# A float32 attention kernel: the transfers of each row maximum are issued by GpSimd instead of SyncE

## The chip, the cores and the metric

The kernel runs on one core of one Trainium2 chip. The metric is the device time of one execution in microseconds (us). Of the kernel before, three timed runs are shown: 7329.24, 7341.15 and 7340.35 us, median 7340.35 us. One more execution was recorded by the hardware profiler. All durations in this document come from that profile unless something else is said.

The engines have short names in the profile: PE is TensorE's matmul, PEld its weight load, DVE is VectorE, ACT is ScalarE, POOL is GpSimd and SP is SyncE. A name with a q behind it (SPq, POOLq) is the engine's queue: issues of transfers and waits for semaphores.

## The reference

The input is x, 4096 rows of 256 numbers, normalised to xn. Two blocks read xn, and the result is x plus both.

The first block is an attention with 16 heads of 16 numbers. It takes most of the time, and the change is in it:

```python
attn = einsum('bqhd,bkhd->bhqk', q, k)
sq = attn * attn
nsum = (qn + kn).transpose(0, 2, 1)[..., None]   # squared lengths of q and k
w = softmax(sq / (nsum - 2.0 * sq + EPS))        # over all 4096 keys
out = einsum('bhqk,bkhd->bqhd', w, v).reshape(B, S, D)
return out @ wo + bo
```

Each of 16 heads has 4096 x 4096 scores, and each score goes through a square, a quotient, an exponential and a matmul with v. The softmax needs the maximum of every row of 4096 scores before its exponential.

The second block has two layers of local attention (8 heads, windows of 128) and a gated feed-forward network. It is called the chain here, since each of its steps follows the one before.

## The kernel before, in words

**Tiles.** The attention is worked in 512 tiles (16 heads x 32 blocks of 128 queries). A tile `i` has 128 queries on the partitions and 4096 keys, in two halves `n = 2i` and `2i + 1` of 2048. A half goes through these methods of the class `Acts`:

- `scores` (L951, PE) and `square` (L955, ACT): products in PSUM, squared into the tile `r`.
- `less` (L959, DVE): subtracts a constant from `r`.
- then the reciprocal of `r` by way of logarithm and exponential: `positive` (L972, DVE), `log` and `power` (L978 and L981, ACT); in some tiles the two halves share one reciprocal, with `product` (L963) and `signed` (L985) on DVE.
- `weights` (L993, DVE): the quotient, and its maximum along the row. After the second half, the maximum over all 4096 keys of each query stands in one column of the small tile `mm` (128 partitions x 1 number).
- `maximum` (L997 to L1007): prepares that maximum for PE. It is the function that is changed.
- `turn` (L1014 and L1017, PE): for each stretch of 512 keys, first a matmul (L1014) that writes minus the row's maximum into PSUM, from the row tile `mrow`; then four transposes (L1017) that add the quotients to it.
- `exp` (L1025, ACT) and `values` (L1036, PE): the exponential of that, and its matmul with v.

**What `maximum` does.** For the matmul L1014, the maxima of 128 queries must lie as a row, along one partition, and in bf16 without loss. So each is split into three bf16 parts. A part is the upper half of the 32-bit number, which `head` shows as bf16; GpSimd subtracts the part from the number (L1007), and the upper half of the rest is the next part. Two subtractions make three parts. Each part, a column of 128 partitions with 2 bytes each, is moved by a transfer (L1004) into one row of `mrow`: row 0, 1 and 2. There are four such tiles (`M_ROWS = 4`), used in turn. Before the change, the transfers are issued by SyncE, in this order for each tile: transfer of part 1, subtraction, transfer of part 2, subtraction, transfer of part 3.

**The order of the work.** PE, ACT and DVE follow an order that a planner (`Plan`, `plan_all`) writes out before the program runs, with a cost in ns for every step; an engine works through its list in order and waits where something isn't there yet. The planner takes `maximum` as 6 us that lie on no engine (`MAX_NS = 6000.0`, "X"): it places a tile's `turn` no earlier than 6 us after the end of its `weights`. The steps of the chain fill the gaps. GpSimd and SyncE have no planned list: they take what the program gives them, in the order of the program, each in its own queue.

**What else lies in these two queues.** SyncE issues nearly all transfers: loads of queries, keys and values of a head (L338, L328, L332), the stores of results (L1045), and the loads and stores of the chain. GpSimd works, besides L1007, for the chain's local attention: in `looked`, four instructions (L745 to L748) split the maxima of a window into bf16 parts in the same manner, 128 times; SyncE moves those (L751) to the row tile `frow`, which PE reads at L760. There are a few fills with constants (L605, L625 to L627, L636) too.

The changed function, as the profile's line numbers have it:

Of the kernel before, what the change touches and what calls it, by code (L numbers as in the profile page):

```python
# [272 lines left out]
def tile_yat_attention_and_local_ffn(ctx: ExitStack, tc: tile.TileContext, io, out):  # L273
    nc = tc.nc
# [648 lines left out]
    class Acts:  # L923
# [74 lines left out]
        def maximum(self, i):  # L998

            mm = self.mm.pop(i)  # L1000
            head = mm.bitcast(BF)
            self.mT[i] = mT = mrow[i % M_ROWS]
            for c_ in range(1, 4):
                nc.sync.dma_start(mT[c_ - 1:c_, :], head[:, 2 * c_ + 1:2 * c_ + 2])  # L1004
                if c_ == 3:
                    break
                G.tensor_tensor(mm[:, c_ + 1:c_ + 2], mm[:, c_:c_ + 1], head[:, 2 * c_ + 1:2 * c_ + 2], ALU.subtract)  # L1007
# [217 lines left out]
```

## Time and profile before

| | |
|---|---|
| timed runs, median of 3 | 7340.35 us (7329.24 to 7341.15) |
| the profiled execution, its own time | 7328.83 us |
| the profiled execution, its span from first to last instruction | 7327.0 us |
| busy: PE, DVE, ACT, POOL | 6747.6, 6907.5, 6972.8, 1806.4 us |
| granted TensorE clock, mean | 0.981 |
| attention tiles from the first L1004 (262.8 us) to the last (7298.7 us) | 512, one in 13.7 us |
| transfers `mrow<-mm` | 1536, of 0.2 KB each |
| instructions L1007 | 1024, 1010 ns in the mean |

How to read it: the first 260 us are a prologue that makes q, k and v. From there on, three engines are busy over 90% of the time, and the chain's work is spread over nearly the whole span. So no single engine's sum is the time; each us in which one of the three waits can show in the end. A mean duration on POOL holds the time in which an instruction had begun and was held up, as the shortest (189 ns) and the longest (11197 ns) of L1007 tell.

### The profile page before, as it was taken

The numbers are of one execution on the slowest core, as the hardware profiler recorded it, in microseconds if no ns is written. First come the engines' busy times: TensorE is split into PE (matmuls) and PEld (weight loads), VectorE is DVE, ScalarE is ACT, GpSimd is POOL, SyncE is SP. The second block draws the span as 40 slices with busy tenths as digits, with TensorE's granted clock in tenths as the row PEclk, the third lists the DMA queues.
The fourth block names the chain that finished last, engine by engine and source line by source line (L and its number), as shares of the span: only waits on it lengthen the run. The fifth ranks groups of instructions, "written<-read, shape, count | busy, mean of one in ns | idle before, by whom it ended". The sixth has DMA issues, their size and how long they took to land. (4 is left out here: it accounts for less than half of the span.)

```text
span 7327.0 us, 158565 instructions
## 1 busy us (share of the span) xinstructions
PE 6747.6 (92%) x66274; PEld 4786.4 (65%) x67136; DVE 6907.5 (94%) x7307; ACT 6972.8 (95%) x6761; POOL 1806.4 (25%) x1567
## 2 busy tenths in 40 slices
PE   7799999999999998899999999999999999999998
PEld 3466666666676665666666676666666666666665
DVE  8999999999999998899999999999999999899998
ACT  8899999999999998899999999999999999899998
POOL 0123233223332322212223322332232220011210
PEclk9899999999999999999999999999999999999999
DMA  3201010010000111011110010101010023101012
GB/s 130 76 16 21 17 24 15 17 22 17 20 19 15 30 40 26 19 31 24 35 21 19 20 19 17 23 14 25 15 23 15 17 59 87 36 21 31 20 46 77
DMA packets 542303, 223.84 MB, mean 31 GB/s; under 512 B 374988, under 2 KB 514003, under 8 KB 539538
## 3 DMA queue, kind: packets, MB, share of 16 engines
q1 hardware_dynamic: 539650, 212.73, 12.3%
q8 instruction: 527, 8.63, 0.5%
q14 instruction: 190, 1.56, 0.1%
q10 hardware_dynamic: 1936, 0.92, 0.0%
HBM read 124.59 MB, written 88.08 MB: 29 GB/s over the span
## 5 line engine op out<-in xcount | busy, mean ns | idle before, releaser
L1017 PE MATMUL pt<-ident,r 128*128 128x128 f32 x16384 | 2497.5, 276 | 0.0
L1017 PEld LDWEIGHTS pt<-ident,r 128*128 128x128 f32 x16384 | 2082.7, 143 | 577.3 <-issue 199.4
L1025 ACT ACTIVATE pe<-pt 128x1024 f32<-128x1024 f32 x2048 | 2178.8, 1099 | 147.0 <-PE pt L1017 122.5
L955 ACT ACTIVATE r<-pt 128x1024 f32<-128x1024 f32 x2048 | 2120.9, 1104 | 86.5 <-PE pt L951 45.0
L1007 POOL TENSOR_TENSOR mm<-mm 128x1 f32<-128x1 f32 x1024 | 1033.9, 1010 | 4714.3 <-DVE mm L993 4547.7
L1014 PE MATMUL pt<-mrow,neg 128*128 128x512 bf16 x4096 | 1577.6, 385 | 220.8 <-DMA mrow<-mm 108.2
L978 ACT ACTIVATE u<-u 128x2048 f32<-128x2048 f32 x702 | 1395.4, 1997 | 26.8 <-DVE u L972 26.4
L981 ACT ACTIVATE u<-u 128x2048 f32<-128x2048 f32 x702 | 1403.5, 1999 | 0.7
L959 DVE TENSOR_SCALAR r<-r 128x2048 f32<-128x2048 f32 x1024 | 1242.5, 1221 | 65.2 <-ACT r L955 64.8
L993 DVE CUSTOM_DVE_ANT_0 r<-r,u,mm 128x2048 f32<-128x2048 f32 x512 | 1201.3, 2346 | 63.4 <-ACT u L981 58.4
L951 PE MATMUL pt<-K,Q 128*128 128x512 bf16 x3234 | 1013.2, 383 | 199.7 <-ACT pe L1025 129.8
L993 DVE CUSTOM_DVE_ANT_0 r<-r,u 128x2048 f32<-128x2048 f32 x512 | 1169.1, 2283 | 13.0 <-ACT u L981 6.4
L1036 PE MATMUL pv<-pe,vh 128*17 128x128 f32 x32768 | 1074.1, 275 | 21.4 <-ACT ob L1043 7.9
L1036 PEld LDWEIGHTS pv<-pe,vh 128*17 128x17 f32 x32768 | 819.0, 97 | 298.7 <-issue 279.7
L985 DVE SCALAR_TENSOR_TENSOR u<-u 128x2048 f32<-128x2048 f32 x322 | 736.1, 2286 | 74.6 <-ACT u L981 73.8
L951 PEld LDWEIGHTS <-Q 128*128 128x128 bf16 x4096 | 375.4, 99 | 574.6 <-issue 393.6
L963 DVE TENSOR_TENSOR u<-r,r 128x2048 f32<-128x2048 f32 x322 | 735.6, 2285 | 1.9
L1014 PEld LDWEIGHTS <-neg 128*128 128x128 bf16 x4096 | 406.7, 99 | 350.7 <-issue 249.6
L972 DVE TENSOR_SCALAR u<-r 128x2048 int32<-128x2048 int32 x380 | 457.1, 1219 | 1.6 <-DMA q_d<-pb 1.5
L972 DVE TENSOR_SCALAR u<-u 128x2048 int32<-128x2048 int32 x322 | 394.4, 1225 | 7.5
L863 PE MATMUL pf<-pT,wqkv_s 128*128 128x512 f32 (+1 forms) x768 | 367.5, 601 | 4.2 <-DVE kv L883 1.5
L745 POOL CAST fm<-mx 128x4 bf16<-128x4 f32 x128 | 216.9, 1695 | 481.2 <-DVE mx L740 470.5
(211 smaller groups left out, 6005.1 us busy)
## 6 DMA issues: line engine op xcount, KB each, us to landing
o<-ob SPq DMA_DIRECT2D x127, 256.0 KB
mrow<-mm SPq DMA_DIRECT2D x1536, 0.2 KB
Q<-q_d SPq DMA_DIRECT2D x256, 48.0 KB
K<-k_d SPq DMA_DIRECT2D x32, 384.0 KB
tab<-in_tables_dram SPq DMA_DIRECT2D x32, 256.0 KB
xres<-xres SPq DMA_DIRECT2D x32, 256.0 KB
xm<-xm SPq DMA_DIRECT2D x32, 256.0 KB
P<-xm SPq DMA_DIRECT2D x32, 256.0 KB
```

Source lines behind the costliest of these rows:

```text
L951: T.matmul(ps[:, j * 512:(j + 1) * 512], lhsT=Q[:, (qt % 4) * 128:(qt % 4 + 1) * 128], rhs=K[:, o + j * 512:o + (j + 1) * 512], start=True ...
L955: A.activation(self.r[n][:, z * 1024:z * 1024 + 1024], self.pt.pop((n, z)), AF.Square)
L959: V.tensor_scalar(self.r[n], self.r[n], 1.0, 1.0e-9, ALU.subtract, ALU.subtract)
L972: V.tensor_scalar(self.part(i, h).bitcast(I32), src.bitcast(I32), 0x7FFFFFFF, None, ALU.bitwise_and)
L978: A.activation(self.part(i, h), self.part(i, h), AF.Ln)
L981: A.activation(self.part(i, h), self.part(i, h), AF.Exp, scale=-2.0)
L993: V.tensor_tensor_reduce(self.r[2 * i + h], self.r[2 * i + h], self.part(i, h), 1.0 if self.paired[i] else -0.5, init, ALU.mult, ALU.max, ...
L1007: G.tensor_tensor(mm[:, c_ + 1:c_ + 2], mm[:, c_:c_ + 1], head[:, 2 * c_ + 1:2 * c_ + 2], ALU.subtract)
L1014: T.matmul(pt[:, 512 * b:512 * b + 512].rearrange("p (s n) -> p s n", s=4), lhsT=neg1, rhs=self.mT[i].unsqueeze(1).broadcast_to([128, 4, 1 ...
L1017: T.matmul(pt[:, 512 * b + j * 128:512 * b + (j + 1) * 128], lhsT=self.r[n][:, o + j * 128:o + (j + 1) * 128], rhs=ident, is_transpose=Tru ...
L1025: A.activation(pe, self.pt.pop((n, z)), AF.Exp)
L1036: T.matmul(pav[32 * (j % 4):32 * (j % 4) + 17, (qt % 4) * 128:(qt % 4) * 128 + 128], lhsT=vh[h % 2][:, kt, :], rhs=pe[:, j * 128:(j + 1) * ...
```

## The change

The three transfers of each tile's maxima are issued on GpSimd's queue in place of SyncE's:

```diff
@@ -1001,7 +1001,7 @@
             head = mm.bitcast(BF)
             self.mT[i] = mT = mrow[i % M_ROWS]
             for c_ in range(1, 4):
-                nc.sync.dma_start(mT[c_ - 1:c_, :], head[:, 2 * c_ + 1:2 * c_ + 2])
+                nc.gpsimd.dma_start(mT[c_ - 1:c_, :], head[:, 2 * c_ + 1:2 * c_ + 2])
                 if c_ == 3:
                     break
                 G.tensor_tensor(mm[:, c_ + 1:c_ + 2], mm[:, c_:c_ + 1], head[:, 2 * c_ + 1:2 * c_ + 2], ALU.subtract)
```

In the built program the lists of PE, DVE and ACT are the same, row for row. SyncE's queue has the 1536 transfers L1004 less, GpSimd's has them more. There a tile is now one run of five instructions: transfer, L1007, transfer, L1007, transfer. The first transfer waits for DVE's maximum, for PE's last read of that `mrow` (four tiles back) and for the transfer eight places back on the same queue; the second and the third wait for the L1007 ahead of them.

## The prediction

> **What bounds the kernel now.** I read the busy times first, then the waits, then one stretch of the timeline.
>
> ```profile
> PE 6747.6 (92%) x66274; PEld 4786.4 (65%) x67136; DVE 6907.5 (94%) x7307; ACT 6972.8 (95%) x6761; POOL 1806.4 (25%) x1567
> ...
> POOL mm L1007 <- DVE mm L993: 4547.7, 432, 23.9
> ...
> ACT pe L1025 <- PE pt L1017: 122.5, 105, 9.9
> ...
> PE pt L1014 <- DMA mrow<-mm: 108.2, 38, 8.8
> ```
>
> The first line (the page) says that ACT, DVE and PE are all nearly full: ACT idles 7327.0 - 6972.8 = 354 us, of which by the trace's records 275 lie between 270 and 7300 us. The others (who waited for whom: total us, times, longest) name the largest wait of ACT for PE, and the largest wait of PE for a transfer: PE at L1014 for the row `mrow`, the very transfers of the change. POOL mostly waits for work. The stretch around 3028 us shows how the last two are one thing:
>
> ```profile
> 3015.16 16.70 POOL L1007 TENSOR_TENSOR mm<-mm 128x1 f32<-128x1 f32 x4 [17.45 <-DVE mm L993]
> ...
> 3028.41 0.59 PE L1014 MATMUL pt<-mrow,neg 128*128 128x512 bf16 x1 [4.57 <-DMA mrow<-mm]
> ...
> 3031.16 1.02 ACT L1025 ACTIVATE pe<-pt 128x1024 f32<-128x1024 f32 x1 [4.86 <-PE pt L1017]
> ```
>
> (Start, us, instruction, idle time before it.) Four subtractions took 16.70 us, the row came late, PE stood 4.57 us, and ACT then stood 4.86 us for PE. That holds at large: the records have 30 stalls of PE over 1.5 us at L1014, 104 us together; in those stretches and the 15 us behind each, ACT idles 142 us where its mean rate would give 22. So I count **a us that PE waits for `mrow` as a us of the span**.
>
> How much room is there? I paired the records tile by tile: the end of DVE's maximum, the three issues, the two L1007, and PE's first L1014. From the maximum to the third issue takes 2.90 us (mean): 0.31 until the first L1007 begins, 1.10 for it, 0.08, 0.92 for the second, 0.50 until SP issues. From the third issue to PE it is never under 2.80 us, and in the tiles that PE waits for it gathers between 2.8 and 3.1; I take 2.9 as the landing. What PE comes later than that is the tile's slack: under 1 us in 47 of 512 tiles, under 2 in 103, under 3 in 179, median 4.2. The added stall of a delay d is the sum of (d - slack) over the tiles whose slack is smaller:
>
> d = 1: 32 us; 2: 105; 3: 242; 3.5: 341; 4: 458; 5: 727; 6: 1051.
>
> A stall shifts the later tiles with it, so their slack stays and the sum holds.
>
> **The change, part by part.**
>
> ```profile
> L1007 POOL TENSOR_TENSOR mm<-mm x1024: 189/1057/11197, 262.9 to 7297.8; 128x1 f32<-128x1 f32 x171
> L1004 SPq DMA_DIRECT2D mrow<-mm x1536: 468/508/1764, 262.8 to 7298.7; - x192
> L745 POOL CAST fm<-mx 128x4 bf16<-128x4 f32 x128 | 216.9, 1695 | 481.2 <-DVE mx L740 470.5 <-DMA mrow<-mm 10.6
> ...
> L959 DVE TENSOR_SCALAR r<-r x1024: 1203/1220/2339, 241.4 to 7273.7; 128x2048 f32<-128x2048 f32 x171
> ```
>
> (Lines of the sources: min/median/max ns; L745 as a group: busy us, mean ns.)
>
> *SyncE loses 1536 issues.* At 0.508 us they are 780 us of a queue that bounds nothing. In the tiles it also takes out SP's lateness: 0.50 us ahead of the third issue. Loads behind a waiting L1004 (queries, `frow`) may start earlier, but no load but `mrow` stands among PE's larger waits, so I count 0 for that; bounded by the L751 issues' 26.5 us behind L1007, it can give at most that.
>
> *GpSimd gains 1536 issues, in series with its subtractions.* Before, the first transfer ran beside the first L1007, and SP issued while POOL subtracted. Now a tile is transfer, L1007, transfer, L1007, transfer in one queue. Let g be POOL's time for one issue. From the maximum to the start of the third: 0.31 + g + 0.08 + 1.10 + 0.05 + g + 0.08 + 0.92 + 0.05 = 2.6 + 2g (0.05 for the step from an L1007 to a transfer). Then the issue, g, and what follows the issue as before, 2.9 - 0.5 = 2.4. So 5.0 + 3g, against 2.90 + 2.9 = 5.8: **d = 3g - 0.8**.
>
> *What is g?* No transfer is issued by POOL before, so it is bounded. From below: the shortest L1007, 0.19 us (then d = -0.2, and the stalled tiles win up to 0.2 us each: 82 of them have over 0.3 us of idle time ahead of L1014, so 16 us). From above: a POOL instruction held up for one long DVE instruction (L963 and L985 take 2.28 us), 2.3 us: d = 6.1, 1088 us. Between: the same transfer costs SP 0.51; POOL's own instructions run from 1.01 (L1007, 128 numbers) to 1.70 us (L745, 512 numbers) in the mean, most of it held up: an L1007 of over 250 ns (560 of 1024) ends some 50 ns after a DVE instruction ended. An issue that spells out 128 pieces of 2 bytes is to me a POOL instruction like these two, so I take the middle, **1.35 us**: d = 3.25, and between the table's 242 and 341 that is 242 + 0.25/0.5 x 99 = **292 us**.
>
> *The chain's maxima behind it.* Queued behind the waiting first transfer on POOL are L745 to L748 of 128 windows, and PE waits for them at L760. A tile's run now holds POOL 3 x 1.35 + 2.0 = 6.1 us in 13.7, so 0.44 of the 128 sets meet it and lose 3 us. The records give `frow` less slack than `mrow`: 3 us for all 128 sets would cost 58 us; 0.44 x 58 = **26 us**. The first transfer's waits for `mrow` four tiles back (55 us) and for the transfer eight places back are long over: PE is never more than 32 us behind the maximum.
>
> *DVE.* Whatever holds POOL up until a DVE instruction ends (a lock, I call it) could hold DVE in turn. 1024 L959 show only one outlier, at 244 us, ahead of the first L1007; so 0 here, and the other end is a rival. PE's, ACT's and DVE's lists don't change.
>
> Sum: 292 + 26 = 318 us. On the profiled execution, 7328.8 + 318 = 7647. Its time is 11.5 below the median of the runs shown, so for a median: **7658 us**, 4.3% slower.
>
> The Trainium skill, DMA: Bandwidth & Descriptors, section Issuing engines are not separate DMA queues, says that transfers from several engines run on the same 16 DMA engines and that a second issuer saves only issue time. In that view little is won by taking 0.508 us issues off SP, which agrees with the first step. Its section Latency and other measured facts has about 0.6 us to the first byte for SyncE's path and about 1 us for GpSimd's; an estimate from this page alone is 0.4 us more per transfer, and as all three come in series, d 1.2 and some 42 us, far less than my sum.
>
> The Trainium skill, SBUF — State Buffer, section SBUF: two separate sides, warns that GpSimd writes the descriptors of its transfers itself and can't while DVE runs in a two-port mode: 620 ns alone, 3100 ns beside such a copy. The trace agrees so far as a held-up L1007 ends with DVE's instruction; no row here shows an issue. An estimate from the page's 3.1 us for every g would be d = 8.5 and a stall of over 2000 us.
>
> **The rivals.**
>
> 1. *GpSimd is starved.* DVE runs without a gap for 10 us at a time, and 28 L1007 took over 4 us. If three more instructions per tile each lose this way, g is 2.3 and the time 7340 + 1088 + some 50 for `frow` = 8480. For it: the 16.70 us above. Against it: half of the L1007 take at most 1.06 us. The wait of PE at L1014 would be by far the largest of the table.
> 2. *DVE is held by GpSimd's issues.* 3 x 1.35 us in 13.7 is 0.30 of the time; 1726 instructions L959 and L972 (1.22 us each; L963 takes 2.28 for as many columns, so I take these for the ones with the lock) would each lose 0.30 x 0.68 = 0.20 us: 350 us on an engine with 372 us of idle time after the prologue, on top of the forecast: up to 8010. Against it: no L959 is stretched today.
> 3. *It is hidden.* If g is about SP's 0.51, d = 0.7, 20 us of stalls, and SP's relief gives as much back: 7345. For it: the median slack of 4.2 us. Against it: g at half of POOL's lightest mean.
> 4. *Faster.* SP is what makes the row late: its first issue comes 0.47 us after the maximum in the mean, its second 0.29 and its third 0.50 after their L1007. If POOL only hands an issue over, d turns negative below **g = 0.27 us**; at 0.19 it wins 16 us, with the 26.5 us of SP's waits up to 43: 7300. Against it: it needs POOL quicker than SP at the same transfer, beside a DVE that is 94% busy.
>
> That the change doesn't do what it says I exclude: the built lists have the 1536 issues on POOL.
>
> **How the numbers follow.** Forecast (moderate stalls, g from 0.6 to 1.9, d from 1.0 to 4.9: 7380 to 8085) 0.58; starved 0.14; DVE held 0.10; hidden 0.10; faster 0.08. Predicted is the first: 7658. The range leaves out the faster case below and the upper half of the starved one: 7330 to 8480, which is the upper bound of g. About 0.2% (15 us) is what a measurement of this kernel can tell from no change: faster by more 0.08, within 0.08 (most of the hidden case), slower by more 0.84.
>
> **What would show it.** In the changed profile, PE's wait at L1014 for `mrow` should grow from 108 (with PEld's 45) to some 400 us and ACT's wait for L1017 with it; ACT's, DVE's and PE's busy times should stay within 1%, so that the loss is all idle time. POOL should show some 2000 us more of work in issues, about 1.3 us each; SP's waits at L1004 should be gone. Busy L959 and L972 above 1.25 us in the mean speak for rival 2, issues over 2 us for rival 1. I am wrong if the span grows without PE waiting for `mrow`, or if issues cost 1.3 us and PE doesn't wait.

## The result, and the profile after

| | before | after |
|---|---|---|
| timed runs, median of 4 | 7340.75 us (7329.24 to 7346.73) | 7563.93 us (7558.85 to 7571.84) |
| ratio | | 1.0308, 95% interval 1.0295 to 1.0321 |
| profiled execution, own time and span | 7328.83 and 7327.0 us | 7571.84 and 7570.1 us |

The kernel became 223 us slower by the medians, 243 us by the two profiled spans. The forecast was 318 us slower.

The page of the changed kernel, its busy times:

```profile
PE 6878.7 (91%) x67136; PEld 4811.6 (64%) x67136; DVE 6918.3 (91%) x7307; ACT 6989.8 (92%) x6761; POOL 3139.4 (41%) x3103
```

ACT and DVE do the same work as before to within 0.3%. (PE's busy time is 131 us more, mostly because the trace of before lacks 862 of PE's 67136 matmul records, all of them L951; in the profile of after all are there. The granted clock was 0.971 after and 0.981 before, and the matmuls L1014 took 388 ns in the mean for 385, L1017 278 for 276: 39 us of busy time together, on an engine that still idles.) So the loss is idle time: between 270 us and the last 30 us, ACT idles 499 us where it idled 273, DVE 604 where it idled 370. Who waited for whom, in the changed kernel (us in total, times, longest):

```profile
PE pt L1014 <- DMA mrow<-mm: 316.5, 130, 9.7
...
ACT pe L1025 <- PE pt L1017: 225.5, 171, 10.7
```

These are the two lines that the prediction put at the centre; they were 108.2 us (38 times) and 122.5 us (105 times). The source lines of the changed function (min/median/max in ns):

```profile
L1004 POOL DMA_DIRECT2D mrow<-mm x1536: 537/572/3645, 262.7 to 7544.2; - x192
...
  POOL mm L1007: 330.5, 972
...
DMA to landing us min/median/max: 2.7/3.2/8.3
```

An issue takes GpSimd 0.54 us at least, 0.81 in the mean; 972 times it begins 0.3 us after a subtraction (330.5 us over 972), and the data land 3.2 us (median) after it began.

One tile of the changed kernel shows where the time goes. Its maximum is ready at 3125.8 us. First GpSimd's timeline, then VectorE's, then the two that wait (start, us, engine, line; in brackets the idle time before):

```profile
3126.33 2.50 POOL L1004 DMA_DIRECT2D mrow<-mm  x1 [12.30 <-PE pt L951]
3128.85 2.12 POOL L1007 TENSOR_TENSOR mm<-mm 128x1 f32<-128x1 f32 x1
3131.27 2.71 POOL L1004 DMA_DIRECT2D mrow<-mm  x1 [0.29 <-POOL mm L1007]
3134.00 2.17 POOL L1007 TENSOR_TENSOR mm<-mm 128x1 f32<-128x1 f32 x1
3136.47 3.25 POOL L1004 DMA_DIRECT2D mrow<-mm  x2 [0.29 <-POOL mm L1007]
```

```profile
3126.37 1.21 DVE L959 TENSOR_SCALAR r<-r 128x2048 f32<-128x2048 f32 x1
3127.51 1.21 DVE L972 TENSOR_SCALAR u<-r 128x2048 int32<-128x2048 int32 x1
3128.64 2.28 DVE L993 CUSTOM_DVE_ANT_0 r<-r,u 128x2048 f32<-128x2048 f32 x1
...
3131.51 1.21 DVE L972 TENSOR_SCALAR u<-r 128x2048 int32<-128x2048 int32 x1
3132.65 1.21 DVE L959 TENSOR_SCALAR r<-r 128x2048 f32<-128x2048 f32 x1
3133.78 2.34 DVE L993 CUSTOM_DVE_ANT_0 r<-r,u,mm 128x2048 f32<-128x2048 f32 x1
```

```profile
3141.53 0.59 PE L1014 MATMUL pt<-mrow,neg 128*128 128x512 bf16 x1 [6.98 <-DMA mrow<-mm]
...
3144.28 1.02 ACT L1025 ACTIVATE pe<-pt 128x1024 f32<-128x1024 f32 x1 [7.26 <-PE pt L1017]
```

Compare the ends of GpSimd's instructions with those of VectorE's. The first issue runs to 3128.83, 0.11 us after L972 ended (3127.51 + 1.21 = 3128.72). The subtraction behind it runs to 3130.97, 0.05 us after L993 ended. The second issue runs to 3133.98, 0.12 us after L959 ended, and the second subtraction again to the end of an L993. Four instructions in one queue, each held up by another instruction of VectorE; the third issue begins 10.7 us after the maximum. PE stands 7 us, and ACT 7 us for PE.

**The parts of the delay**, from the records paired tile by tile (means, us). Where a SyncE transfer landed is read from the updates of its semaphore: eight semaphores take turns, each transfer adds sixteen updates, and the last one before that semaphore's next transfer is the landing. In the 36 tiles of the kernel before where PE waits over 1 us for the row, it starts 0.04 to 0.14 us after the landing so read.

| | before | after |
|---|---|---|
| maximum to the first issue | 0.47, beside the subtraction | 0.77 |
| first issue | | 0.81 |
| maximum to the first L1007 | 0.31 | 1.60 |
| first L1007 | 1.10 | 1.24 |
| to the second L1007 | 0.08 | 1.23 (0.38, an issue, 0.02) |
| second L1007 | 0.92 | 1.07 |
| to the third issue | 0.50 | 0.30 |
| third issue to landing | 3.83 | 3.41 |
| maximum to the whole row | 6.73 | 8.85 |

The row comes 2.12 us later. The prediction took 2.9 us for SyncE's landing, which is near its shortest (2.73) and not its mean; the expectations below took it over, and so speak of a row that comes 3.05 us later.

### The profile page after: what moved, and what is told of

Read it like the earlier page. It is cut to its first block, busy times and chain, and to the rows that moved or that the text cites. A ratio compares the mean times of both kernels' runs of the same rounds, so it can differ in the third digit from the quotient of the medians.

```text
span 7570.1 us, 158759 instructions
## 1 busy us (share of the span) xinstructions
PE 6878.7 (91%) x67136; PEld 4811.6 (64%) x67136; DVE 6918.3 (91%) x7307; ACT 6989.8 (92%) x6761; POOL 3139.4 (41%) x3103
## 3 DMA queue, kind: packets, MB, share of 16 engines
q1 hardware_dynamic: 318466, 212.24, 10.2%
q0 software_dynamic: 49152, 0.49, 0.5%
q14 instruction: 184, 1.51, 0.1%
## 5 line engine op out<-in xcount | busy, mean ns | idle before, releaser
L1004 POOL DMA_DIRECT2D mrow<-mm x1536 | 1246.0, 811 | 3818.3 <-issue 1256.3
L1017 PE MATMUL pt<-ident,r 128*128 128x128 f32 x16384 | 2524.1, 278 | 0.0
L1017 PEld LDWEIGHTS pt<-ident,r 128*128 128x128 f32 x16384 | 2102.8, 144 | 556.6 <-issue 181.2
L1025 ACT ACTIVATE pe<-pt 128x1024 f32<-128x1024 f32 x2048 | 2149.2, 1079 | 265.5 <-PE pt L1017 225.5
L955 ACT ACTIVATE r<-pt 128x1024 f32<-128x1024 f32 x2048 | 2095.8, 1085 | 154.2 <-PE pt L951 153.2
L1014 PE MATMUL pt<-mrow,neg 128*128 128x512 bf16 x4096 | 1590.0, 388 | 439.4 <-DMA mrow<-mm 316.5
L978 ACT ACTIVATE u<-u 128x2048 f32<-128x2048 f32 x702 | 1381.6, 1976 | 22.9 <-DVE u L972 22.4
L981 ACT ACTIVATE u<-u 128x2048 f32<-128x2048 f32 x702 | 1388.7, 1978 | 0.7
L959 DVE TENSOR_SCALAR r<-r 128x2048 f32<-128x2048 f32 x1024 | 1242.9, 1221 | 85.8 <-ACT r L955 85.6
L993 DVE CUSTOM_DVE_ANT_0 r<-r,u,mm 128x2048 f32<-128x2048 f32 x512 | 1200.7, 2345 | 66.8 <-ACT u L981 61.3
L951 PE MATMUL pt<-K,Q 128*128 128x512 bf16 x4096 | 1139.8, 384 | 125.6 <-ACT pe L1025 91.9
L1007 POOL TENSOR_TENSOR mm<-mm 128x1 f32<-128x1 f32 x1024 | 1179.8, 1152 | 20.0
L993 DVE CUSTOM_DVE_ANT_0 r<-r,u 128x2048 f32<-128x2048 f32 x512 | 1168.5, 2282 | 15.2 <-ACT u L981 6.8
L985 DVE SCALAR_TENSOR_TENSOR u<-u 128x2048 f32<-128x2048 f32 x322 | 735.7, 2285 | 110.6 <-ACT u L981 109.6
L1014 PEld LDWEIGHTS <-neg 128*128 128x128 bf16 x4096 | 408.6, 100 | 618.1 <-issue 529.0
L963 DVE TENSOR_TENSOR u<-r,r 128x2048 f32<-128x2048 f32 x322 | 735.2, 2283 | 1.9
L951 PEld LDWEIGHTS <-Q 128*128 128x128 bf16 x4096 | 377.6, 99 | 550.4 <-issue 375.9
L972 DVE TENSOR_SCALAR u<-r 128x2048 int32<-128x2048 int32 x380 | 457.9, 1220 | 1.6 <-DMA q_d<-pb 1.5
L972 DVE TENSOR_SCALAR u<-u 128x2048 int32<-128x2048 int32 x322 | 394.5, 1225 | 7.5
```

Of the source, the lines that this page charges most:

```text
L951: T.matmul(ps[:, j * 512:(j + 1) * 512], lhsT=Q[:, (qt % 4) * 128:(qt % 4 + 1) * 128], rhs=K[:, o + j * 512:o + (j + 1) * 512], start=True ...
L955: A.activation(self.r[n][:, z * 1024:z * 1024 + 1024], self.pt.pop((n, z)), AF.Square)
L959: V.tensor_scalar(self.r[n], self.r[n], 1.0, 1.0e-9, ALU.subtract, ALU.subtract)
L978: A.activation(self.part(i, h), self.part(i, h), AF.Ln)
L981: A.activation(self.part(i, h), self.part(i, h), AF.Exp, scale=-2.0)
L993: V.tensor_tensor_reduce(self.r[2 * i + h], self.r[2 * i + h], self.part(i, h), 1.0 if self.paired[i] else -0.5, init, ALU.mult, ALU.max, ...
```

## The experiments

Two theories were put against each other. **Late row**: the loss is PE waiting for a row that comes later, whatever makes it late. **Issue**: the loss comes from GpSimd's issues as such (VectorE held, the other queue of transfers, the chain's maxima behind them). All times are medians, and the ratios are against runs of the kernel before taken beside them; diffs are against the kernel before unless said otherwise.

### The row late without an issue by GpSimd

```diff
-                self.mm[i] = hp.tile([128, 4], F32, name="mm", bufs=4)
+                self.mm[i] = hp.tile([128, 8], F32, name="mm", bufs=4)
...
             head = mm.bitcast(BF)
+            for x_ in range(4, 7):
+                G.tensor_tensor(mm[:, x_:x_ + 1], mm[:, 1:2], head[:, 3:4], ALU.subtract)
```

> The transfers stay on SyncE as before; three more subtractions on GpSimd, which nothing uses, stand ahead of the two real ones, so that the second and third part come some 3 x 1.1 = 3.3 us later while no transfer is issued by GpSimd. Theory 'late row' (the loss is PE waiting for a row that comes 3.05 us later): PE's wait at L1014 grows from 108 to 300 us or more and the time to 7540 to 7600. Rival 'issue' (the loss comes from GpSimd's issues themselves: DVE held, the software queue of transfers, the chain's maxima behind them): no more than 7400.

Measured: 7596.48 us, ratio 1.0349 (1.0332 to 1.0366). Its waits:

```profile
PE pt L1016 <- DMA mrow<-mm: 293.6, 89, 11.5
ACT pe L1027 <- PE pt L1019: 283.9, 171, 12.5
```

(L1016, L1019 and L1027 are before's L1014, L1017 and L1025.) With no issue on GpSimd, the loss is there, and it stands in the same two lines. That speaks for the late row. One number did not come as expected: the third issue is only 1.55 us later in the mean (4.45 against 2.90 us after the maximum) and the row 1.46 us (8.19 against 6.73), yet the loss is as large as in the changed kernel. The mean hides the tail: in one tile in a hundred the third issue now comes over 16.8 us after the maximum (before 10.4). The sum of (delay - slack), with the landings as recorded, is 127 us for 1.46 us in every tile, and 267 us with each tile's own delay; PE's idle time ahead of a tile's first L1014 grew by 232.

### The issues without a late row, twice

```diff
+    mdup = [cp.tile([3, 128], BF, name=f"mdup{i}") for i in range(M_ROWS)]
...
+            for c_ in range(1, 4):
+                nc.gpsimd.dma_start(mdup[i % M_ROWS][c_ - 1:c_, :], head[:, 2 * c_ + 1:2 * c_ + 2])
```

> The transfers stay on SyncE as before; GpSimd issues the same three transfers once more, after both subtractions, into tiles that nothing reads. The row is not later, but GpSimd's 1536 issues and their queue are there. Theory 'late row': 7320 to 7380, the wait of PE at L1014 within 50 us of before's 108. Rival 'issue': 7480 or more, DVE's busy time or its idle time up without PE waiting for the row.

Measured: 7877.86 us, ratio 1.0734 (1.0718 to 1.0750). Neither theory as stated: the time is beyond the rival's, but the loss isn't where the rival looked for it. PE waits for the row again (L1017 is here what is L1014 in the kernel before):

```profile
PE pt L1017 <- DMA mrow<-mm: 459.9, 154, 16.5
```

Yet SyncE's third issue is only 0.56 us later. In the tiles whose wait is over 1 us, PE begins 7.7 us (median) after the third issue; in the kernel before 3.1. The row *lands* late: over all tiles SyncE's third transfer needs 7.01 us in the mean, before 3.83. GpSimd's are slow too (see the first fence below). The records of the transfers' packets say where: the last 2-byte packet of SyncE's third transfer ends 1.63 us after the issue in the mean, before 1.48. So the packets are taken up nearly as early as ever, and what has grown lies between them and the semaphore. The next kernel asks whether the place of landing makes that:

```diff
+    mdup = [cp.tile([128, 128], BF, name=f"mdup{i}") for i in range(M_ROWS)]
...
+            for c_ in range(1, 4):
+                nc.gpsimd.dma_start(mdup[i % M_ROWS][79 + c_:80 + c_, :], head[:, 2 * c_ + 1:2 * c_ + 2])
```

> As e2_dup_issue, but the copies that nothing reads land in rows 80, 81 and 82 of their tiles, not in rows 0, 1 and 2, where mrow's parts land too. e2 made 7878 us, because the real rows landed later (PE's shortest time from the third issue to L1014 went from 2.8 us to 5 us and more), though their issues were as early as before. Theory 'same rows': six transfers of 2-byte pieces into the same few partitions wait for each other at the place of landing; apart, the landing returns to some 3 us and the time to 7350 to 7420 (one issue between the two subtractions makes the row 0.6 us later, 15 to 20 us). Rival 'same queues': they wait for each other in the transfer engines or at the column mm that both read, wherever they land: 7800 or more again.

Measured: 7397.13 us, ratio 1.0078 (1.0065 to 1.0092). GpSimd's transfers, first in the kernel where they land in rows 0 to 2, then in the one with rows 80 to 82:

```profile
DMA to landing us min/median/max: 2.8/6.6/16.4
```

```profile
DMA to landing us min/median/max: 2.8/3.8/12.0
```

The rows alone make 481 us of difference, and SyncE's third transfer is back at 3.73 us. And 1536 issues by GpSimd cost 60 us where the landing is free of them, as much as PE's idle time ahead of L1014 grew (202 us against 142): one issue stands between the two subtractions, and the row is there 0.66 us later. The issues as such are cheap.

### More room in the plan

```diff
-MAX_NS = 6000.0
+MAX_NS = 9000.0
```

On the changed kernel:

> The changed kernel with MAX_NS 9000 in place of 6000: the planner places a tile's transposes 3 us later, as much as the row is later. Theory 'late row': PE's wait at L1014 falls from 316 to 130 us or less, the time to 7300 to 7400. Rival 'issue': still 7500 or more. Read beside the kernel before with the same 9000, since the other plan may cost or win something by itself.

On the kernel before:

> The kernel before with MAX_NS 9000. Theory 'late row': nearly no wait of PE at L1014 (under 40 us), so up to 110 us less than before, 7230 to 7340, if the later place costs nothing elsewhere (nine r tiles are held longer); the changed kernel with 9000 lies no more than 100 us above it. Rival 'issue': the two with 9000 lie 200 us or more apart.

Measured: 7378.42 us (1.0055, 1.0040 to 1.0070) and 7310.93 us (0.9962, 0.9947 to 0.9977). The changed kernel's row is as late as ever (9.08 us after the maximum), but PE comes for it later:

```profile
PE pt L1014 <- DMA mrow<-mm: 133.4, 59, 10.9
```

On the kernel before, the wait fell from 108 to 54.0 us, not under 40 as expected. The change costs 67 us with this plan, where it cost 223 with the other. So 156 us of the loss were lateness against the plan; the rest too is for the most part PE's remaining wait (183 us of idle time ahead of L1014 against 101 in its twin).

### One transfer alone

```diff
-                nc.sync.dma_start(mT[c_ - 1:c_, :], head[:, 2 * c_ + 1:2 * c_ + 2])
+                (nc.gpsimd if c_ == 3 else nc.sync).dma_start(mT[c_ - 1:c_, :], head[:, 2 * c_ + 1:2 * c_ + 2])
```

> The third transfer alone goes to GpSimd. Theory 'late row', by the parts measured in the changed kernel: its issue begins 0.30 us after the second subtraction (0.50 on SyncE) and lands 3.41 us later (2.9): d = 0.3 us, 6 to 10 us of stalls, 7340 to 7360. Rival 'issue' (a third of the loss goes with a third of the issues): 7415.

and with `c_ == 1`:

> The first transfer alone goes to GpSimd, ahead of both subtractions. Theory 'late row': the first subtraction begins 1.60 us after the maximum, not 0.31: d = 1.0 to 1.3 us, 32 to 45 us of stalls, 7365 to 7400. Rival 'issue': 7415, the same as for the third alone.

Measured: third alone 7363.64 us (1.0035, 1.0021 to 1.0049), first alone 7385.90 us (1.0063, 1.0051 to 1.0076). The first alone came as the late row has it: the first subtraction begins 1.62 us after the maximum. The third alone costs 27 us, a little more than expected: its issue begins 0.32 us after the subtraction (0.50 on SyncE), but lands 4.08 us later, where GpSimd's needed 3.41 in the changed kernel and SyncE's 3.83 before. The row is 0.18 us later with the third alone and 1.05 with the first alone, together over half of the 2.12, and their 76 us are a third of the loss: stalls grow faster than the delay, as the prediction's table of slack says.

### One issue less ahead of the subtractions

Against the changed kernel:

```diff
-            for c_ in range(1, 4):
-                nc.gpsimd.dma_start(mT[c_ - 1:c_, :], head[:, 2 * c_ + 1:2 * c_ + 2])
-                if c_ == 3:
-                    break
+            for c_ in range(1, 3):
                 G.tensor_tensor(mm[:, c_ + 1:c_ + 2], mm[:, c_:c_ + 1], head[:, 2 * c_ + 1:2 * c_ + 2], ALU.subtract)
+            for c_ in range(1, 4):
+                nc.gpsimd.dma_start(mT[c_ - 1:c_, :], head[:, 2 * c_ + 1:2 * c_ + 2])
```

> All three transfers on GpSimd, but its queue is subtraction, transfer, subtraction, transfer, transfer: one issue less ahead of the subtractions. Theory 'late row': 1.3 us of the 3.05 are won back, d = 1.7 to 1.9, 80 to 100 us of stalls, 7420 to 7460. Rival 'issue': as many issues as in the changed kernel, so 7560.

Measured: 7516.51 us (1.0245, 1.0231 to 1.0259). It won 47 us back, under half of what I expected. The third issue comes 1.2 us earlier (4.22 us after the maximum), but its landing takes 4.20 us, not 3.41, with the second issue 0.80 us ahead of it and not 2.2; the row is there after 8.42 us, 1.69 later than before. The sum of (delay - slack) with the landings as recorded is 161 us for 1.69, and 180 were measured. So the theory holds, and my number for the landing was wrong.

### Rows apart

```diff
-    G.memset(neg1, 0.0)
-    G.memset(neg1[0:3], -1.0)
+    G.memset(neg1, -1.0)
...
-                nc.sync.dma_start(mT[c_ - 1:c_, :], head[:, 2 * c_ + 1:2 * c_ + 2])
+                nc.sync.dma_start(mT[40 * (c_ - 1):40 * (c_ - 1) + 1, :], head[:, 2 * c_ + 1:2 * c_ + 2])
```

> The kernel before, with the three parts of a maximum landing in rows 0, 40 and 80 of mrow, not 0, 1 and 2 (neg1 is -1 in all rows; the other rows of mrow are 0, so the sums stay). Theory 'same rows' (from e2_dup_issue and e2b_dup_apart: transfers of 2-byte pieces into neighbouring rows slow each other's landing): SyncE's three overlap only in part, so the landing after the third issue (shortest 2.8 us) falls by up to 0.3 us: 7320 to 7345. Rival (only software and hardware queues together slow each other): 7335 to 7345.

The same rows in the changed kernel:

> The changed kernel with the same rows 0, 40 and 80. Theory 'same rows': the third landing falls from 3.41 us in the mean towards the first's 2.8 to 3.0, d from 3.05 to 2.5 us, 75 to 85 us less: 7470 to 7500. Rival: the three issues are 2 us apart and no longer overlap much; the 3.41 us is the software queue's own, and the time stays at 7550 to 7570.

Measured: 7295.74 us (0.9946, 0.9934 to 0.9959) with SyncE's issue, 7559.58 us (1.0306, 1.0292 to 1.0320) with GpSimd's. On SyncE, where the issues are close together, it wins 39 us, which lies below both ranges: the third landing fell from 3.83 to 2.93 us in the mean, and in tiles that wait over 1 us, three quarters have PE start within 2.97 us of the third issue (before 4.60). On GpSimd the issues lie over 2 us apart; the third landing only fell from 3.41 to 3.24 us, and the time stays. There the rival was right.

### Without GpSimd

The loop keeps its three transfers on SyncE, and the subtractions move into `weights`:

```diff
             if h:
                 del self.u[i]
+                mm, head = self.mm[i], self.mm[i].bitcast(BF)
+                for c_ in range(1, 3):
+                    V.tensor_tensor(mm[:, c_ + 1:c_ + 2], mm[:, c_:c_ + 1], head[:, 2 * c_ + 1:2 * c_ + 2], ALU.subtract)
...
-                if c_ == 3:
-                    break
-                G.tensor_tensor(mm[:, c_ + 1:c_ + 2], mm[:, c_:c_ + 1], head[:, 2 * c_ + 1:2 * c_ + 2], ALU.subtract)
```

> The kernel before with the two subtractions on DVE, right behind the maximum, so that GpSimd and its waits for DVE are out of the row's way. Theory 'late row': the third issue comes 1.3 us after the maximum (now 2.90), PE's idle time ahead of L1014 falls from 142 to 60 us or less; DVE gets 1024 small instructions of some 0.08 us (its own L993 read of the maximum takes 0.08), 80 us, of which some or all shows: 7260 to 7340. Rival (PE's waits for the row are made elsewhere, and the row's lateness only covers them): 7400 or more, by DVE's added work and no gain.

Measured: 7333.32 us, ratio 1.0002 (0.9992 to 1.0011). PE's idle time ahead of L1014 fell to 70 us (60 or less expected), but a subtraction takes DVE 159 ns, twice my guess:

```profile
L999 DVE TENSOR_TENSOR mm<-mm x1024: 159/159/178, 262.8 to 7300.8; 128x1 f32<-128x1 f32 x171
```

That is 163 us more on an engine with 370 us of idle time, of which 222 are left; 72 us of PE's waits are gone, and the time is the same, so the added work seems to cost about what the waits gave back. The row is there after 6.16 us, only 0.57 earlier than before, though the third issue comes 1.57 us after the maximum and not 2.90: its landing now takes 4.59 us.

### The fastest

Rows apart on SyncE, with `MAX_NS = 8000.0`:

> SyncE's issue, rows 0, 40 and 80 (e9_before_rows, 7296 us) and MAX_NS 8000 in place of 6000. Theory 'late row': e9 has 117 us of idle time of PE ahead of L1014 left; with two us more room it falls to some 60, and the time to 7240 to 7290. Rival (e9 has taken what e4's later place took too): 7290 to 7310.

Measured: 7287.30 us, ratio 0.9939 (0.9926 to 0.9953), faster than both kernels. The time lies in the theory's range, but not for the theory's reason: PE still idles 115 us ahead of L1014, not 60. Against the rows apart alone the intervals overlap, and the later place adds nothing that these runs can tell, as the rival said.

### What the runs say together

| kernel | PE idle ahead of a tile's first L1014, us | more than before | time more than before, us |
|---|---|---|---|
| before | 142 | | |
| changed | 373 | +231 | +223 |
| changed, rows apart | 366 | +224 | +224 |
| changed, subtraction first | 312 | +170 | +180 |
| changed, 9 us of room | 183 | +41 | +38 |
| first transfer alone | 206 | +64 | +49 |
| third transfer alone | 169 | +27 | +27 |
| three idle subtractions | 374 | +232 | +256 |
| copies into rows 80 to 82 | 202 | +60 | +60 |
| copies into rows 0 to 2 | 582 | +440 | +537 |
| before, 9 us of room | 101 | -41 | -30 |
| rows apart on SyncE | 117 | -25 | -39 |
| rows apart, 8 us of room | 115 | -27 | -45 |

(The idle time is of the profiled execution, from the records; the times are medians.) In eleven of these twelve kernels the time follows this one wait to within 24 us; the copies into rows 0 to 2 lose 97 us more than the wait grew. The subtractions on DVE, which are not in the table, are the exception by design: that kernel loses 72 us of it and seems to pay them with DVE's own time.

## Why the prediction was right

1. *A us of PE waiting for `mrow` is a us of the span.* Right: the table above.
2. *The delay, d = 3g - 0.8 = 3.25 us.* Too large: 2.12 was measured. The mis-sized term is SyncE's landing in the kernel before, taken as 2.9 us because the tiles that PE waits for were said to gather between 2.8 and 3.1. They don't: of the 36 with over 1 us, half lie above 3.12 us and a quarter above 4.60. The mean over all tiles is 3.83, so the old row is there after 6.73 us and not 5.8. For the new row the formula has 9.05 us and 8.85 were measured, but by luck. g is 0.81 us, not 1.35 (GpSimd's busy time grew by 1333 us, not some 2000). Against that, the first issue begins 0.77 us after the maximum (0.31 assumed); 0.38 and 0.30 us pass between a subtraction and the issue behind it (0.05); the subtractions take longer (2.31 us for 2.02); what follows the third issue takes 2.6 us, not 2.4. Two errors of over a us met.
3. *The stall for that delay, 292 us.* The slack was counted with the same 2.9 us, so it was too large as well: with the landings as recorded, 105 tiles have under 1 us of it (the prediction has 47) and 178 under 2 (103). The same sum then gives 235 us for 2.12 us in every tile, and 274 with each tile's own delay. The measured growth is 231 us. So the method holds to within a fifth. That 292 us came so near is luck too: a delay taken too long was set against slack taken too large.
4. *The chain's maxima, 26 us.* Mis-sized too: PE waits for `frow` 0.8 us in all, by the profile of that tile. L745 to L748 did not get slower either (1.39 us in the mean, before 1.51). If sets that meet a tile's run came later, PE hardly waited for them.
5. *DVE at 0, SyncE at 0.* Right: L959 takes 1221 ns in the mean in both, and its row after is the one before but for a few ns; no other load shows among PE's larger waits.

```profile
L959 DVE TENSOR_SCALAR r<-r x1024: 1203/1220/2335, 240.7 to 7512.6; 128x2048 f32<-128x2048 f32 x171
```

Of the 318 us, some 60 were too much in terms 2 and 3 by the measured stall, and 26 in term 4.

Rival 1, starvation, happens in single tiles like the one shown (the longest issue is 3.6 us), but not in the mean. Rival 3 had g nearly right (0.51 against 0.54 at the shortest) and failed on the 0.3 us steps and the waits for DVE. Rival 4's turning point, g = 0.27, is half of the shortest issue; with SyncE's landing as recorded the same formula turns at 0.58 us, just above the shortest.

The skill's warning can now be read in the trace. The Trainium skill, SBUF — State Buffer, section SBUF: two separate sides, says that GpSimd's writing of descriptors is blocked by VectorE in a two-port mode until its end and some 115 ns; its subsection Who interferes with whom adds, as an inference, that an instruction with two inputs takes only the read side, which such writing does not need. Of 259 issues that begin beside an L972, 249 take over 800 ns, and of 393 beside an L959, 183; of 317 beside L963, L985 or L993, the instructions with two inputs, none. None of the first 652 ends before the VectorE instruction that it began beside; all of the 317 do. The long ones end some 118 ns (median) after a VectorE instruction. So the trace agrees. The page's 620 ns alone and 3100 beside a copy are told of a whole transfer; here the issue alone took 537 ns at the shortest, 3645 at the longest, 811 in the mean.

## What to carry to other kernels

Before a transfer is moved to the engine that makes its data, count what that engine's queue then does in series: here two issues of 0.8 us stepped in front of two short instructions that had run beside them. Measure the slack of the consumer item by item and sum (delay - slack) over the late ones; that sum, with the consumer on a path where three engines are full, was 235 to 274 us where PE's wait grew by 231. Read the landings themselves for it: the one number that was taken from the shortest case, 2.9 us for 3.83, was the one that bent both the delay and the slack. And where a plan assumes a latency, the plan is the first thing to change with it: the same change cost 67 us in place of 223 when the plan knew of 3 us more.

## What the runs showed of the hardware that was not expected

- Transfers of 128 pieces of 2 bytes into neighbouring rows of one tile, or of another tile in the same rows, slow each other's landing across queues: median 6.6 us for GpSimd's with six in rows 0 to 2, 3.8 us with its three in rows 80 to 82; the times differ by 481 us. With SyncE alone, rows 0, 40 and 80 in place of 0, 1 and 2 brought the third landing from 3.83 to 2.93 us and made the kernel 0.54% faster. The time is lost behind the packets: in both pairs the last one ends 1.48 to 1.63 us after the issue in the mean. Whether it is the row itself or a path that neighbouring rows share was not tried. The Trainium skill, SBUF — State Buffer, section Door 1: The DMA port swizzle, puts partitions 0 to 3 and 32 to 35 behind one port of the transfers, and 40 and 80 behind two others. The runs fit that, but don't show it: rows 0, 32 and 35 (one port by the page, rows apart) would tell it from the rows.
- The two queues cut the same transfer differently. SyncE's queue has 539650 packets before and 318466 after, 221184 less for 1536 transfers, 144 each (128 of 2 bytes and 16 of 4); GpSimd's queue has 49152, 32 each (16 of 16 bytes and 16 of 4). SyncE's queue before and after, then GpSimd's after:

```profile
q1 hardware_dynamic: 539650, 212.73, 12.3%
```

```profile
q1 hardware_dynamic: 318466, 212.24, 10.2%
q0 software_dynamic: 49152, 0.49, 0.5%
```

- GpSimd's take less of the transfer engines' time: 0.5% of it, where SyncE's queue lost 2.07 ms of packet time, 1.8% of sixteen engines over the span before. They don't land sooner by themselves: 3.27 us for the first transfer against SyncE's 3.05, and with rows apart 3.24 against 2.93 for the third. With neighbouring rows SyncE's third, issued 1.2 us behind the second, takes 3.83, and GpSimd's, 2.2 us behind, 3.41.
- A subtraction of 128 numbers takes DVE 159 ns where reading out its own maximum (L993) takes 82.
